# A gated graph network and an attention layer on one core: the work ahead of the first block in another order, W's extra columns in four steps, two products of v and W at a time, and both aggregation halves in one tick

## The chip, the cores and the metric

The kernel runs on one core of a Trainium2 chip. The metric is the device time of one execution in microseconds (us), lower is better. A profile is a recording of one execution; its span goes from the first to the last instruction, and the execution's own time lies a little above it.

## The reference

There are 64 graphs of 256 nodes with 256 features. A first layer runs three gated steps with a shared GRU cell and adds its input; a second layer is a masked attention over the neighbours. Each is followed by a layer norm.

```python
A = (adj != 0)
h = x
for i in range(3):
    m = h @ weight[i]
    aggr = einsum('bst,bsd->btd', A, m)
    h = gru_cell(aggr, h, w_ih, w_hh, b_ih, b_hh)
x = layernorm(x + h)
Wh = x @ W
e = leaky_relu((Wh @ a1)[:, :, None] + (Wh @ a2)[:, None, :], 0.2)
attn = softmax(where(adj > 0, e, -9e15), axis=2)
out = layernorm(x + attn @ Wh)
```

with `r = sigmoid(i_r + h_r)`, `z = sigmoid(i_z + h_z)`, `n = tanh(i_n + r * h_n)` and the new state `(1 - z) * n + z * h` in the cell.

## The kernel before

**Tiling.** P is 128, C = 2 chunks of 128 nodes or features, G = 2 graphs make a pair, so there are 32 pairs, and K = 4 chunks of nodes in a pair. The state of a pair is held turned, features on partitions: `hT` is 128 by 2 by 512. Since the adjacency comes first in the products, the kernel folds each `weight[i]` with `w_ih` into one weight, `wc[i]`, and aggregates the state itself.

**Three products for one.** To keep precision with the fast matmul type, an operand is cut into a high part, a low part and a cross part (`pieces`, tags H, L and D): `upper` on ScalarE (line 132), `lower` as a subtraction on VectorE or GpSimd (line 135), `cross` on VectorE (line 138). For a weight, `cut_weight` (line 140) also scales the low part on GpSimd (line 149), through a temporary `cut`. Ahead of clock 0 the temporary has three buffers; later, one (the tag `wh` of the pool `late`).

**Ticks.** The order of the work is written out by hand. There is a clock of ticks and a heap of steps that fall due: `at(t, step)` puts one in, `tick()` advances the clock and runs what is due, in order of the tick and then of entry. A step only issues instructions; each engine works through its own queue in that order, and semaphores make it wait for the others. The step's place in the tick order is thus its place in five queues at once.

**Blocks.** A block is layer i of pair p (lines 845 to 847); three pairs are under way at a time, in layers 0, 1 and 2, one after the other. `gates(p, i, lags)` (line 456) issues a block's products (line 468): for each half of the output columns r, n, z and t, each of 4, 6 or more matmuls of 512 columns from the H, L and D parts, into two PSUM banks `pga` and `pgb`, with one tick between the parts and one at the end, so 12 ticks in a block. ScalarE (line 473 and 475) and VectorE (line 477) bring the two banks together; sigmoid and tanh (line 486) and GpSimd (lines 494 to 504) finish the gate, and VectorE writes the new state (line 507).

**The front of the next block** is issued in the ticks of the one before: `front(p, i, t, pace)` (line 385). Its steps, for each half d: `turn` (transposes, lines 280 and 369), `split` (the high part on ScalarE, line 405), `rest` (the low part, line 135), `aggregate` (8 matmuls of 256 columns into a bank `pa`, line 439), `a_upper` (aH on ScalarE) and `a_rest` (aL and aD on VectorE). The step's tick is t plus its entry in `pace` plus d, so the two halves come one tick apart. Three more, `h_upper`, `h_lower` and `h_cross`, make hH, hL (on GpSimd) and hD. The paces are the tuples CLOSE, EARLY, FIRST, SECOND and THIRD at lines 832 to 836.

**PSUM** is one pool of eight banks (`bank`, line 106), taken in turn.

**Ahead of the first block** (lines 855 to 876) the clock runs from -100. Pair 0's x is turned and split, `rows_T` (line 214) turns the rows of w_ih and w_hh into `wihT` and the pieces `whh`, `square_T` (line 222) turns weight[0] into `wT`, `ones` (line 376) makes A of pair 0's adjacency, `fold` (line 234) makes `wc[0]` in four parts (two column ranges of 512 and 256, two halves d), and the front of pair 0 runs among them. Then the clock is set to 0 and the blocks begin. The folds of layers 1 and 2 and `attention_rows` are issued as steps in the first blocks: layer i's transposes at tick 8i-7, its halves 2 and 5 ticks later, and `attention_rows` at tick 17.

**attention_rows** (line 242) makes W's two extra columns, W times a1 and a2, and takes the mean over the rows from W: transposes of `gw` into `gwT` (line 226 and the copy at 229), four matmuls of 2 columns (line 247) with their copies (line 249), a memset of `mean` (line 251), two matmuls against it (line 254) and two subtractions (line 256). It is one step: all of it is issued together.

**attention(p, t)** (line 546) is issued in the ticks after a pair's last layer. `project(k)` (line 581) multiplies chunk k of the turned input by `gw`, 258 columns at the full type, into a bank `pwh` (line 589), at tick t+37+k. `spread(k)` (lines 598 and 600) takes it out of the bank one tick later, on ScalarE for k = 0 and 1 and on VectorE for 2 and 3. The last three pairs have their own version, `attention_last`.

Of the kernel before, what the change touches and what calls it, by code (L numbers as in the profile page):

```python
# [19 lines left out]
P = 128  # L20
# [7 lines left out]
def kernel(  # L28
# [60 lines left out]
    def at(t, step):  # L89
        clock[1] += 1  # L90
        heappush(pending, (t, clock[1], step))
# [14 lines left out]
    def bank(name):  # L106
        return psum.tile([P, 512], F32, tag="bank", name=name)
# [83 lines left out]
    w_n = []  # L191
# [30 lines left out]
    def square_T(src, name):  # L222
        pt = bank("pw")
        for e in range(C):
            for d in range(C):
                nc.tensor.transpose(pt[:, (e * C + d) * P:(e * C + d + 1) * P],
                                    src[:, d, e * P:(e + 1) * P], ident)
        dst = work.tile([P, GN], F32, tag="z", name=name)
        nc.scalar.copy(dst, pt)
        return dst.rearrange("p (e d) -> p e d", e=C)  # L230
# [8 lines left out]
                                 start=(e == 0), stop=(e == C - 1))  # L239
            cut_weight([t[:, d, o0:o1] for t in wc[i]], pt[:, :o1 - o0], f"{i}_{d}_{o0}")  # L240

    def attention_rows():
        gwT = square_T(gw, "gwT")
        for d in range(C):
            pt = bank("pw")
            for f in range(C):
                nc.tensor.matmul(pt[:, :2], gwT[:, f, d * P:(d + 1) * P], a_w[:, :, f],
                                 start=(f == 0), stop=(f == C - 1))
            nc.vector.tensor_copy(gw[:, d, D:], pt[:, :2])
        mean = late.tile([P, C, GN], F32, tag="vT", name="mean")[:, 0, :P]  # L250
        nc.vector.memset(mean, 1.0 / D)
        pt = bank("pw")[:, :D + 2]
        for d in range(C):
            nc.tensor.matmul(pt, mean, gw[:, d, :], start=(d == 0), stop=(d == C - 1))
        for d in range(C):
            nc.vector.tensor_sub(gw[:, d, :], gw[:, d, :], pt)


    class Pair:
# [125 lines left out]
    def front(p, i, t, pace):  # L385

        nm = f"{p}_{i}"
        by_dma = getattr(pairs.get(p), "by_dma", None) == i
        hi, lo, src = [None] * C, [None] * C, [None] * C
        if by_dma:  # L390
            hi, lo = pairs[p].hi, pairs[p].lo

        def turn(d):
            s = pairs[p]
            if i == 0:
                if p < FROM:
                    to_T(s.x, s.hT, d)
            else:
                src[d] = from_T(s.hT, d).rearrange("p (k n) -> p k n", k=K)

        def split(d):
            if i == 0:
                src[d] = nodes(pairs[p].x, d)
            hi[d] = work.tile([P, K, P], F32R, tag=f"hi{d}", name=f"hi{d}_{nm}", bufs=1)
            nc.scalar.copy(hi[d], src[d])

        def rest(d):
            lo[d] = work.tile([P, K, P], F32R, tag=f"lo{d}", name=f"lo{d}_{nm}", bufs=1)
            lower(nc.gpsimd if i == 0 and p else nc.vector, lo[d], src[d], hi[d])

        def stash():
            s = pairs[p]
            s.far = far.tile([P, C, GN], F32, tag="xT", name=f"xT_{p}")
            nc.sync.dma_start(s.far, s.hT)
        if i == 0:
            at(t + pace[0][0] + 3, stash)

        def h_upper():
            s = pairs[p]
            s.hc = pieces(work, [P, C, GN], nm, "h")  # L420
# [125 lines left out]
    def attention(p, t):  # L546
# [305 lines left out]

    def rows_inp(part):
        rows_T(part, lambda c, o0, o1, pt: evacuate(wih(c, o0, o1), pt))
    begin(0)
# [94 lines left out]
```

## Time and profile before

| What | Value |
|---|---|
| Median of 3 runs | 2078.24 us (2077.84 to 2080.43) |
| The profiled execution's own time | 2080.38 us |
| Its span | 2078.6 us |
| TensorE matmuls busy | 2048.2 us, 9844 instructions |
| TensorE weight loads busy | 1724.7 us |
| VectorE busy | 1787.8 us |
| ScalarE busy | 1659.6 us |
| GpSimd busy | 1616.4 us |
| Mean granted TensorE clock | 0.995 |
| Moved by DMA | 254.28 MB |

The page's parts, as the later sections use them: the first part gives the busy time of each engine (PE is TensorE's matmul, PEld its weight load, DVE VectorE, ACT ScalarE, POOL GpSimd, SP the queue that issues most DMAs); the second cuts the span into 40 slices, busy tenths of each, with the clock that TensorE was granted; the list of waits says for how long an engine sat idle ahead of a kind of instruction, whose end it waited for, how often, and the longest. A timeline row has its start and duration in us, the engine, the line in the kernel, what is written from what, the shapes and the number of merged instructions; in square brackets stands the idle time before it and who ended it. A matmul's busy time reaches into the next one's, so the distance from start to start is what a matmul costs. Two records of TensorE belong to one matmul at the full type (the folds and the products of v and W).

### The profile page before, as it was taken

Reading aid. Unit: us, or ns where it says so; the run is one execution under the profiler, and the core shown is the slowest. Engines: PE = TensorE matmul, PEld = TensorE weight load, DVE = VectorE, ACT = ScalarE, POOL = GpSimd, SP = SyncE. Lnnn points to the kernel's source line nnn. Section 1 sums busy time; section 2 is a strip of 40 time slices with the busy share of each in tenths; the row PEclk is TensorE's granted clock in tenths of the full one; section 3 lists DMA queues with packets and bytes.
Section 4 is the critical chain, followed back from the end, with each engine's and each line's share of the span. In section 5 each row is a group of like instructions: output and inputs, shape, how many; then the busy total and the mean of one; then the engine's idle time right before and its main releaser. Section 6 shows DMA issues by size and latency. Waiting matters only on the chain.

```text
span 2078.6 us, 31369 instructions
## 1 busy us (share of the span) xinstructions
PE 2048.2 (99%) x9844; PEld 1724.7 (83%) x9844; DVE 1787.8 (86%) x2896; ACT 1659.6 (80%) x3025; POOL 1616.4 (78%) x1114
## 2 busy tenths in 40 slices
PE   8999999999999999999999999999999999999996
PEld 6788888888888888888888888888888888888885
DVE  5676888898888898888898888898888898888887
ACT  4566888888888888888888888888888888888775
POOL 6777878787878787878787878787878787878763
PEclk9999999999999999999999999999999999999998
DMA  4112465664666665665665666665666665666221
GB/s 132 37 51 58 92 137 136 144 141 122 133 138 136 143 141 121 133 139 136 144 134 128 133 138 137 143 142 121 133 137 137 143 136 126 128 144 137 62 62 61
DMA packets 549734, 254.28 MB, mean 122 GB/s; under 512 B 372608, under 2 KB 541312, under 8 KB 549568
## 3 DMA queue, kind: packets, MB, share of 16 engines
q1 hardware_dynamic: 547776, 250.44, 54.9%
q8 instruction: 78, 1.28, 0.3%
q10 hardware_dynamic: 1616, 1.57, 0.2%
q14 instruction: 88, 0.72, 0.1%
q0 software_dynamic: 176, 0.27, 0.1%
HBM read 69.74 MB, written 33.55 MB: 50 GB/s over the span
## 4 chain that ended last, share of the span: by engine, by line
PE 96%; DVE 1%; POOL 1%; ACT 1%; DMA 0%; issue 0%; POOLq 0%; ACTq 0%; SPq 0%; DVEq 0%
PE pga L468 50%; PE pgb L468 25%; PE pa L439 9%; PE pwh L589 5%; PE po L673 5%; PE s L608 1%; PE pt L369 1%; PE pw L238 0%; DMA rows_hH<-in_L_gnn_w_hh_dram 0%; PE pwh L733 0%; PE po L796 0%; POOL wc2L_wc L149 0%; DVE cut L135 0%; PE pw L219 0%; POOL t L494 0%
## 5 line engine op out<-in xcount | busy, mean ns | idle before, releaser
L494 POOL TENSOR_TENSOR t<-hT,n 128x512 f32<-128x512 f32 x192 | 264.1, 1375 | 186.2 <-ACT n L486 185.9
L500 POOL TENSOR_TENSOR n<-n,r 128x512 f32<-128x512 f32 x192 | 318.5, 1659 | 74.8 <-ACT r L486 45.0
L504 POOL TENSOR_TENSOR n<-n,t 128x512 f32<-128x512 f32 x192 | 284.7, 1483 | 110.4 <-DVE t L477 100.6
L468 PE MATMUL pga<-hH,whhH_whh 128*128 128x512 f32 x1152 | 370.6, 403 | 0.0
L468 PE MATMUL pgb<-hD,whhD_whh 128*128 128x512 f32 x1152 | 356.9, 391 | 1.2 <-DVE hD L138 1.2
L468 PE MATMUL pga<-hL,whhL_whh 128*128 128x512 f32 x1152 | 356.9, 391 | 0.0
L495 POOL TENSOR_TENSOR t<-t,z 128x512 f32<-128x512 f32 x192 | 271.1, 1412 | 15.1
L135 POOL TENSOR_TENSOR hL<-hT,hH 128x1024 fp32r<-128x1024 f32 x96 | 260.5, 2714 | 9.1 <-ACT hH L132 9.0
L468 PEld LDWEIGHTS pgb<-hD,whhD_whh 128*128 128x128 f32 x1152 | 216.4, 188 | 49.0 <-DVE hD L138 1.5
L468 PEld LDWEIGHTS pga<-hL,whhL_whh 128*128 128x128 f32 x1152 | 216.5, 188 | 47.1
L468 PEld LDWEIGHTS pga<-hH,whhH_whh 128*128 128x128 f32 x1152 | 208.7, 189 | 35.0
L138 DVE SCALAR_TENSOR_TENSOR hD<-hH,hT 128x1024 fp32r<-128x1024 f32 x96 | 203.2, 2117 | 0.0
L486 ACT ACTIVATE n<-n,bi 128x512 f32<-128x512 f32 x192 | 139.0, 724 | 75.9 <-POOL n L504 75.6
L473 ACT ACTIVATE r<-pga 128x512 f32<-128x512 f32 x192 | 114.0, 594 | 103.6 <-PE pga L468 68.4
L439 PE MATMUL pa<-A,hi 128*128 128x256 f32 x768 | 194.3, 286 | 0.0
L439 PE MATMUL pa<-A,lo 128*128 128x256 f32 x768 | 192.0, 283 | 0.0
L507 DVE TENSOR_TENSOR hT<-t,n 128x512 f32<-128x512 f32 x192 | 191.1, 995 | 0.0
L477 DVE SCALAR_TENSOR_TENSOR r<-pgb,r 128x512 f32<-128x512 f32 x192 | 131.9, 687 | 60.5 <-PE pgb L468 32.2
L135 DVE TENSOR_TENSOR aL<-pa,aH 128x512 fp32r<-128x512 f32 x192 | 131.0, 682 | 59.6 <-ACT aH L132 59.5
L132 ACT ACTIVATE aH<-pa 128x512 fp32r<-128x512 f32 x192 | 116.1, 606 | 67.3 <-PE pa L439 67.3
L486 ACT ACTIVATE z<-z,b_sum 128x512 f32<-128x512 f32 x192 | 140.7, 733 | 19.6 <-DVE z L477 19.1
L473 ACT ACTIVATE t<-pga 128x512 f32<-128x512 f32 x192 | 115.6, 602 | 45.7 <-PE pga L468 41.9
(172 smaller groups left out, 5411.8 us busy)
## 6 DMA issues: line engine op xcount, KB each, us to landing
adj<-in_adj_dram SPq DMA_DIRECT2D x64, 512.0 KB, 3.8
second_h<-first_h SPq DMA_DIRECT2D x220, 128.0 KB, 4.1
x<-in_x_dram SPq DMA_DIRECT2D x32, 512.0 KB, 3.8
xT<-hT SPq DMA_DIRECT2D x32, 512.0 KB, 4.5
vT<-xT SPq DMA_DIRECT2D x32, 512.0 KB, 3.4
second<-first SPq DMA_DIRECT2D x116, 128.0 KB, 3.1
second<-v SPq DMA_DIRECT2D x116, 128.0 KB, 3.9
sc<-eT SPq DMA_DIRECT2D x232, 64.0 KB, 2.2
```

Source lines behind the costliest of these rows:

```text
L135: eng.tensor_sub(dst, src, hi.bitcast(F32))
L138: nc.vector.scalar_tensor_tensor(dst, hi.bitcast(F32), 1.0 + U, src, op0=ALU.mult, op1=ALU.subtract)
L439: nc.tensor.matmul(pt[:, g * N:(g + 1) * N], h[:, g * C + c, :], s.A[:, g, c, :], start=(n == 0), stop=(n == len(todo) - 1))
L468: nc.tensor.matmul(pt, w[:, d, o * P:(o + 1) * P], m[:, d, :], start=n in (0, ends + 1), stop=n in (ends, len(todo) - 1))
L473: nc.scalar.activation(dst, a, AF.Copy, scale=1.0 + U)
L477: nc.vector.scalar_tensor_tensor(dst, b, -1.0 / U, dst, op0=ALU.mult, op1=ALU.add)
L486: nc.scalar.activation(dst, dst, func, bias=bias)
L494: nc.gpsimd.tensor_sub(t, h, n)
L495: nc.gpsimd.tensor_mul(t, t, z)
L500: after(2, lambda r=r, n=n: nc.gpsimd.tensor_mul(n, n, r))
L504: after(1, lambda n=n, t=t: nc.gpsimd.tensor_add(n, n, t))
L507: after(lags[2], lambda n=n, t=t, h=h: nc.vector.tensor_add(h, t, n))
```

## The change

Four parts of the program are edited.

1. `attention_rows` becomes a tuple of four steps, `rows_turned`, `rows_times`, `rows_mean` and `rows_less`, which hand their tiles on in a dict. They are due at ticks 17, 18, 21 and 21.
2. In `front`, for layers 1 and 2 the steps `aggregate`, `a_upper` and `a_rest` aren't due before the tick of the second half's aggregation, so both halves' aggregations are issued in one tick; `a_upper` and `a_rest` keep their ticks or come in that one. Layer 0 keeps its paces.
3. In `attention`, `project(0)` and `project(1)` are issued at t+37, `project(2)` and `project(3)` at t+39. `spread` keeps its ticks, and `attention_last` isn't touched.
4. Ahead of the first block, every step is put into the heap with a tick of its own instead of standing between calls of `tick`, with other paces for pair 0's front, and what is not yet due at the end is moved to the new clock. The transposes of the second part of w_hh come before those of the second part of w_ih. Layer 1's fold does both halves at tick 3, and layer 2's starts at tick 7, with its halves at 12 and 16.

```diff
-    def attention_rows():
-        gwT = square_T(gw, "gwT")
+    rows_of = {}
+
+    def rows_turned():
+        rows_of["T"] = square_T(gw, "gwT")
+
+    def rows_times():
         for d in range(C):
-            pt = bank("pw")
+            pt = rows_of[d] = bank("pw")
...
-        mean = late.tile([P, C, GN], F32, tag="vT", name="mean")[:, 0, :P]
+
+    def rows_mean():
+        mean = rows_of["mean"] = late.tile([P, C, GN], F32, tag="vT", name="mean")[:, 0, :P]
...
+    def rows_less():
         for d in range(C):
-            nc.vector.tensor_sub(gw[:, d, :], gw[:, d, :], pt)
+            nc.vector.tensor_sub(gw[:, d, :], gw[:, d, :], rows_of["m"])
+    attention_rows = rows_turned, rows_times, rows_mean, rows_less
...
-                at(t + dt + d, lambda step=step, d=d: step(d))
+                dt = dt + d
+                if i and step in (aggregate, a_upper, a_rest):
+                    dt = max(dt, pace[0][3] + 1)
+                at(t + dt, lambda step=step, d=d: step(d))
...
         for k in range(K):
-            at(t + 37 + k, lambda k=k: project(k))
+            at(t + 37 + k // 2 * 2, lambda k=k: project(k))
             at(t + 37 + 1 + k, lambda k=k: spread(k))
...
-    front(0, 0, clock[0] + 1, ((0, 1, 2, 9, 11, 12), (7, 8, 13)))
-    tick(2)
-    rows_inp(wi_n[0])
-    tick()
-    rows_hid(wh_n[0])
-    tick()
-    rows_inp(wi_n[1])
-    tick()
-    rows_hid(wh_n[1])
-    wT = square_T(w_n[0], "wT_0")
-    nc.vector.tensor_add(b_sum, bi, bh)
-    tick()
-    ones(0)
-    load_adj(1)
-    tick()
-    for parts in PARTS:
+    front(0, 0, clock[0] + 1, ((0, 0, 1, 9, 11, 12), (5, 6, 10)))
+    for n, part in enumerate(wi_n):
+        after((3, 5)[n], lambda part=part: rows_inp(part))
+    for n, part in enumerate(wh_n):
+        after((4, 4)[n], lambda part=part: rows_hid(part))
+    after(5, lambda: wTs.update({0: square_T(w_n[0], "wT_0")}))
+    after(5, lambda: nc.vector.tensor_add(b_sum, bi, bh))
+    after(5, lambda: ones(0))
+    after(5, lambda: load_adj(1))
+    for n, o in enumerate(PARTS):
         for d in range(C):
-            fold(0, wT, d, (parts,))
-            tick(2)
-    tick(10)
-    load_x(1)
+            after((7, 14)[n] + 2 * d, lambda o=o, d=d: fold(0, wTs[0], d, (o,)))
+    after(17, lambda: load_x(1))
+    tick(25)
+    while pending and pending[0][0] <= clock[0]:
+        run_due()
+    moved = [(t - clock[0], n, step) for t, n, step in pending]
+    pending[:] = sorted(moved)
     clock[0] = 0
-    wTs = {}
...
-    for i in range(1, L):
-        after(8 * i - 7, lambda i=i: start_fold(i))
-        for d in range(C):
-            after(8 * i - 5 + 3 * d, lambda i=i, d=d: fold(i, wTs[i], d))
-    after(8 * L - 7, attention_rows)
+    for i, (t0, t1, t2) in enumerate(((0, 3, 3), (7, 12, 16)), 1):
+        after(t0, lambda i=i: start_fold(i))
+        after(t1, lambda i=i: fold(i, wTs[i], 0))
+        after(t2, lambda i=i: fold(i, wTs[i], 1))
+    for t0, step in zip((17, 18, 21, 21), attention_rows):
+        after(t0, step)
```

More of the change, by code (lines that the diff above doesn't have):

```diff
@@ L240, in fold @@
             cut_weight([t[:, d, o0:o1] for t in wc[i]], pt[:, :o1 - o0], f"{i}_{d}_{o0}")
-    def attention_rows():
-        gwT = square_T(gw, "gwT")
+    rows_of = {}
+    def rows_turned():
+        rows_of["T"] = square_T(gw, "gwT")
+    def rows_times():
         for d in range(C):
-            pt = bank("pw")
+            pt = rows_of[d] = bank("pw")
             for f in range(C):
-                nc.tensor.matmul(pt[:, :2], gwT[:, f, d * P:(d + 1) * P], a_w[:, :, f],
+                nc.tensor.matmul(pt[:, :2], rows_of["T"][:, f, d * P:(d + 1) * P], a_w[:, :, f],
                                  start=(f == 0), stop=(f == C - 1))
             nc.vector.tensor_copy(gw[:, d, D:], pt[:, :2])
-        mean = late.tile([P, C, GN], F32, tag="vT", name="mean")[:, 0, :P]
+    def rows_mean():
+        mean = rows_of["mean"] = late.tile([P, C, GN], F32, tag="vT", name="mean")[:, 0, :P]
         nc.vector.memset(mean, 1.0 / D)
-        pt = bank("pw")[:, :D + 2]
+        pt = rows_of["m"] = bank("pw")[:, :D + 2]
         for d in range(C):
             nc.tensor.matmul(pt, mean, gw[:, d, :], start=(d == 0), stop=(d == C - 1))
+    def rows_less():
         for d in range(C):
-            nc.vector.tensor_sub(gw[:, d, :], gw[:, d, :], pt)
+            nc.vector.tensor_sub(gw[:, d, :], gw[:, d, :], rows_of["m"])
+    attention_rows = rows_turned, rows_times, rows_mean, rows_less
     class Pair:
@@ L854, in rows_inp @@
         rows_T(part, lambda c, o0, o1, pt: evacuate(wih(c, o0, o1), pt))
+    wTs = {}
     begin(0)
     take_x(0)
-    front(0, 0, clock[0] + 1, ((0, 1, 2, 9, 11, 12), (7, 8, 13)))
-    tick(2)
-    rows_inp(wi_n[0])
-    tick()
-    rows_hid(wh_n[0])
-    tick()
-    rows_inp(wi_n[1])
-    tick()
-    rows_hid(wh_n[1])
-    wT = square_T(w_n[0], "wT_0")
-    nc.vector.tensor_add(b_sum, bi, bh)
-    tick()
-    ones(0)
-    load_adj(1)
-    tick()
-    for parts in PARTS:
-        for d in range(C):
-            fold(0, wT, d, (parts,))
-            tick(2)
-    tick(10)
-    load_x(1)
+    front(0, 0, clock[0] + 1, ((0, 0, 1, 9, 11, 12), (5, 6, 10)))
[8 more added lines that the diff above has]
+    for n, o in enumerate(PARTS):
+        for d in range(C):
+            after((7, 14)[n] + 2 * d, lambda o=o, d=d: fold(0, wTs[0], d, (o,)))
[5 more added lines that the diff above has]
+    pending[:] = sorted(moved)
     clock[0] = 0
-    wTs = {}
     def start_fold(i):
         wTs[i] = square_T(w_n[i], f"wT_{i}")
-    for i in range(1, L):
-        after(8 * i - 7, lambda i=i: start_fold(i))
-        for d in range(C):
-            after(8 * i - 5 + 3 * d, lambda i=i, d=d: fold(i, wTs[i], d))
-    after(8 * L - 7, attention_rows)
+    for i, (t0, t1, t2) in enumerate(((0, 3, 3), (7, 12, 16)), 1):
[4 more added lines that the diff above has]
+        after(t0, step)
     for n, (p, i) in enumerate(blocks):
```

## The prediction

> **What bounds the kernel now.** I read the page's first two parts, then the waits of TensorE, then its timeline at both ends of the longest waits.
>
> ```profile
> PE 2048.2 (99%) x9844; PEld 1724.7 (83%) x9844; DVE 1787.8 (86%) x2896; ACT 1659.6 (80%) x3025; POOL 1616.4 (78%) x1114
> PEclk9999999999999999999999999999999999999998
> ```
>
> TensorE is the bound from end to end; a gain must shorten its work, close a gap of it, or raise its clock. Its waits name nine gaps; these matter here:
>
> ```profile
> PE pw L247 <- ACT gwT L229: 2.3, 1, 2.3
> PE pw L219 <- DMA rows_hH<-in_L_gnn_w_hh_dram: 1.3, 1, 1.3
> PE pgb L468 <- DVE hD L138: 1.2, 1, 1.2
> PE pga L468 <- DVE aL L135: 1.0, 1, 1.0
> PE pw L238 <- ACT wT L229: 0.7, 1, 0.7
> PE pw L254 <- DVE mean L251: 0.4, 1, 0.4
> ```
>
> None repeats: all lie in the first 70 us, the stretch that the diff rewrites. (The three left out are x's first load, 6.0, and 7.5 us in the last pairs, which the diff leaves alone.) The timeline of TensorE around two of them:
>
> ```profile
> 24.93 0.47 PE L468 MATMUL pga<-aL,wc0L_wc 128*128 128x512 f32 x1
> 26.36 0.47 PE L468 MATMUL pga<-aL,wc0L_wc 128*128 128x512 f32 x1 [0.95 <-DVE aL L135]
> 27.99 0.74 PE L468 MATMUL pgb<-hD,whhD_whh 128*128 128x512 f32 x2 [1.17 <-DVE hD L138]
> ...
> 31.05 1.05 PE L468 MATMUL pga<-hL,whhL_whh 128*128 128x512 f32 x2
> 31.91 0.70 PE L468 MATMUL pgb<-hD,whhD_whh 128*128 128x512 f32 x2
> ```
>
> The reader is to see two things. A busy duration overlaps the next, so loss is read from start to start: 24.93 to 26.36 is 1.43 where a product normally takes 0.23. And after the gaps, two products start 0.86 us apart from the next two (31.05 to 31.91) where 0.455 is normal. The stretches of 3.41 us show why (columns: busy us of PE, PEld, DVE, ACT, POOL, then the granted clock):
>
> ```profile
> 25.25:28.66 3.41, 1.29 (x5) 0.76 (x5) 3.41 (x6) 2.17 (x4) 3.25 (x3) 1.00 0.00 0
> 28.66:32.07 3.41, 3.41 (x12) 2.73 (x11) 1.66 (x2) 0.00 (x0) 0.42 (x1) 0.50 0.35 77
> ...
> 66.21:69.62 3.41, 1.44 (x10) 1.32 (x11) 0.46 (x3) 0.59 (x1) 2.13 (x2) 1.00 0.00 0
> 69.62:73.03 3.41, 3.41 (x12) 2.73 (x11) 1.89 (x4) 0.59 (x1) 0.00 (x0) 0.50 0.00 0
> ```
>
> Each stretch in which TensorE worked under half the time is followed by one at half clock. So an early gap is paid twice.
>
> [...] a stretch with 2.73 of 3.41 busy, from 15.01, was followed by full clock. [...] the half-clock stretches count as 3.41 of 3.41 busy. [...] both halves of pa were complete by about 21.6, yet aH began at 22.79, behind wc0H at 22.51. [...] hD[...] took 1.22 us at 26.72 and 2.12 on average; I use both ends.
>
> **The change part by part.** I compare the order of instructions of the two programs with durations from the trace.
>
> *First block.* TensorE's order is unchanged up to the first aL product; what moves is who stands ahead on the other queues.
> - ScalarE now does hH before the first wc0H: it starts about 16.0, in a gap that ScalarE has anyway (2.07 us before wc0H at 18.02). It does both aH before the 256-wide wc0H: about 20.7 and 21.7 instead of 22.79.
> - GpSimd: hL (2.37) goes ahead of the first wc0L. The whhL steps end between 18.4 and 19.4, hL thus between 20.8 and 22.2[...]; needed at 23.64. The two 512-wide wc0L (1.5 each) end by 23.7 to 25.2; the second is needed at 25.16.
> - VectorE: wc0D ends at 21.73; then hD (1.22 to 1.9), which before stood last, then aL, aD, aL, aD at 0.61 each. hD ends at 22.9 to 23.6 (needed 25.4, before 27.94); the second aL at 24.8 to 25.4 (needed 25.16, before 26.21); the last aD at 25.4 to 26.0 (needed 26.07). The four 256-wide cut steps (0.34 start to start) now come after, and are wanted only by the n product, microseconds later.
> - SP: its order stays; A comes some 0.8 us earlier as the second lo (1.14) leaves its place, so adj and x of pair 1 are issued no later than 18.66 and 19.14.
>
> Removed: 1.43-0.23 = 1.20 and (27.99-26.36)-0.23 = 1.40; left: 0 to 0.3. The gap at hH's DMA (1.3) and wT (0.7) stay: hL's rows move ahead of aL's on TensorE, but hH's load lands at 10.95 and wT's copy at 15.96 in either order.
>
> *Folds of W.* Layer 1's second fold comes at once after the first, layer 2's later. The TensorE work is the same; the cover is the pair's products. The temporary of a cut has one buffer, so each cut waits for GpSimd: four rounds of about 2.2, 1.3, 2.2, 1.3 = 7 us, and n's combination on VectorE is queued behind them, holding its PSUM bank. The folds start near 28.4 and run 5.2 us (twice the 2.6 from 32.44 to 35.02), to 33.6; the first is copied by 30.9, so the rounds end near 37.9. The last bank comes round after four transposes, 18 products and eight aggregation matmuls: 33.6+0.4+4.1+1.0 = 39.1. Cost nothing, with 1.2 us of cover; without it, what is over, up to 1 us.
>
> *W's extra columns.* Before, transposes, copy, products, mean and subtraction stand together, and gwT's copy waits for a z buffer (GpSimd's t, 1.5 us): last transpose 65.19, next matmul 67.79, so 2.60-0.11 = 2.49, and 0.4 for mean. In the new order, ten matmuls (four transposes and six products, 1.8 us) lie between gwT's transposes and its use, enough for a copy of 0.59 and its queue. The mean's memset (0.17) now stands on VectorE behind r's combination, and its two matmuls follow the n product directly: 0 to 0.7 lost, I take 0.6.
>
> Stalls: removed 1.20+1.40+2.49+0.4 = 5.5; left 0.6; **4.9 us gained**, between 3.5 and 5.5.
>
> *Clock.* Work in a half-clock stretch takes double, so each costs 3.41/2 = 1.7 us. With at most 0.6 us idle at a place, neither stretch is near the rows that tripped it: **3.4 us gained**; 1.7 if one trips still, 0 if both.
>
> *Products and aggregation halves together.* The products after a group of eight aggregation matmuls start 0.47, 0.46, 0.46 us apart per two, then 0.455: 0.03 us lost per break. A pwh group plus three such pairs takes 1030.17 to 1032.42 = 2.25, less 3x0.455 and four matmuls at 0.216: 0.02 lost. In the new order there are 57 fewer pwh breaks and 35 fewer aggregation breaks (where layer 1's first half stood next to the s2 transposes, it leaves one break there): 57x0.02+35x0.03 = 2.2. The trace shows no group of double length between products in the steady stretch, so this is bounded by 0 (the recovery doubles too) and 2.2; I take **1.5**. A slower end is excluded unless a bank or input is late, which is a rival below. spread stays on its ticks, so the second product's bank is held one tick longer; TensorE has no bank wait in the trace, and the bank comes round only after seven others.
>
> Sum: 4.9+3.4+1.5 = 9.8 us, against the profiled execution's 2080.38 (span 2078.6 and 1.8 around): 2070.6. That run is 2.1 above the median of three, 2078.24, about one half-clock stretch; if the median run had one fewer, it would gain 8.1 and end at 2070.1. I predict **2070.0**.
>
> **Rivals.**
> 1. *The stall moves on.* hL, wc0L and aL are within 0.3 us of late[...]. If two of them wait about 1.2 us in one stretch and the clock halves once, 2x1.2+1.7 = 4.1 come back: 2074.1. For: GpSimd is busy 3.25 of 3.41 us there. Against: hL gains at least 1.2 us.
> 2. *The gain is hidden anyway*: the pair's elementwise chain, not TensorE, ends the first blocks, and what TensorE gains it waits later. Only the 1.5 remain: 2076.7. Against: no TensorE wait from 73 us to the last pairs.
> 3. *Slower*: the first aggregation half now comes one tick (about 2.3 us) later, so ScalarE and VectorE get two halves at once, and aL or aD misses the next block. Per turn, layer 1's last aD ends at 1049.80 and its first product starts at 1053.36, layer 2's at 1072.32 against 1075.16: slack 2.8 to 3.6. Only the earlier half moves, so it would take a further 2.8 us of delay; at 0.3 us beyond, in 62 turns, 18.6 lost: 2070.0+18.6 = 2088.6. It turns the sign from 0.16 us a turn.
> 4. *It doesn't group*: excluded, the instruction order shows it.
>
> **How the numbers follow.** Forecast 0.76 (2066.5 to 2074); rival 1 0.10; rival 2 0.08; rival 3 0.06. The low end is all upper bounds: 5.5+3.4+2.2 = 11.1 off 2078.24 is 2067.1, and 0.6 for the runs' own spread. The high end takes in rival 1's edge, 2074.5. A measurement tells 0.2%, 4.2 us, from no change: faster means below 2074.1. Forecast and a third of rival 1 are faster (0.79); the rest of rival 1 and rival 2 the same (0.15); rival 3 slower (0.06).
>
> **What would show it.** Right: no TensorE wait on aL, hD or gwT over 0.4 us; no 0.50 clock between 20 and 100 us; aH near 20.7; hL done before 22.3; product steps back at 0.455 after a group of sixteen with one break of 0.03. Wrong: a wait on wc0L or hL near 25, on mean near 70 over 1 us, a half-clock stretch there, or any TensorE wait repeated every turn.

## The result and the profile after

| | Median, us | Runs |
|---|---|---|
| before | 2080.01 (2077.82 to 2082.54) | 14 |
| after | 2075.66 (2074.62 to 2078.32) | 14 |
| ratio | 0.998 (95%: 0.9972 to 0.9988) | |

The changed kernel is faster by 4.35 us, a fifth of a per cent. The forecast was 2070.0, from 2066.5 to 2074.5, with a gain of 8 to 10 us: the sign is right, the size half of it or less. (The kernel before, which had a median of 2078.24 in the three runs known ahead, has 2080.01 in fourteen.) The profiled execution after took 2075.49, its span 2073.7. Each median below is set against runs of before on the same chip; a difference of means is given with its standard error.

In the kernel after, `gates` is at L480 (before L468), `aggregate` at L448, the products of v and W at L601, the rows steps at L251 to L264. The page's first lines after:

```profile
PE 2045.1 (99%) x9844; PEld 1721.6 (83%) x9844; DVE 1786.0 (86%) x2896; ACT 1659.6 (80%) x3025; POOL 1615.7 (78%) x1114
PEclk9999999999999999999999999999999999999998
```

TensorE is the bound as before; its busy time counts half-clock stretches as busy (3.41 of 3.41 us in the one from 2047.95, below) and so tells little of the change. Its waits after, without x's first load and two in the last pairs:

```profile
PE pt L796 <- ACT sc L784: 4.4, 7, 1.5
PE pw L219 <- DMA rows_hH<-in_L_gnn_w_hh_dram: 1.3, 1, 1.3
PE pw L260 <- DVE mean L257: 1.2, 1, 1.2
PE pga L480 <- POOL wc0L_wc L149: 0.9, 1, 0.9
PE pw L238 <- ACT wT L229: 0.7, 1, 0.7
PE pw L219 <- DMA rows_hL<-in_L_gnn_w_hh_dram: 0.4, 1, 0.4
```

The waits on aL, hD and gwT are gone. Two of about 1 us stand there now, on wc0L (new) and on mean (0.4 before), and a shorter one on hL's DMA. Their places in TensorE's timeline:

```profile
23.55 0.48 PE L480 MATMUL pga<-aL,wc0L_wc 128*128 128x512 f32 x1
24.93 0.50 PE L480 MATMUL pga<-aL,wc0L_wc 128*128 128x512 f32 x1 [0.91 <-POOL wc0L_wc L149]
25.27 0.62 PE L480 MATMUL pgb<-hD,whhD_whh 128*128 128x512 f32 x2
...
69.54 0.62 PE L480 MATMUL pgb<-hD,whhD_whh 128*128 128x512 f32 x2
71.32 1.11 PE L260 MATMUL pw<-gw,mean 128*128 128x258 f32 x4 [1.16 <-DVE mean L257]
```

From start to start, 24.93 - 23.55 - 0.23 = 1.15 us are lost at the first and 71.32 - 69.54 - 0.46 = 1.32 at the second. The stretches of 3.41 us, windows from here on, are those at whose borders the granted clock changes: in the trace of before at 15.01, 28.66, 32.07, 69.62, 73.03 and 2045.94, thus 4, 1, 11, 1 and 578 times 3.413 us apart. The ones that hold the two waits and two of the tail (busy us of PE, PEld, DVE, ACT, POOL; then the clock, and the DMA's share and GB/s):

```profile
23.83:27.24 3.41, 2.50 (x13) 1.94 (x13) 3.21 (x7) 2.21 (x4) 3.17 (x4) 1.00 0.02 5
27.24:30.65 3.41, 3.41 (x14) 2.17 (x13) 0.06 (x1) 1.28 (x2) 1.18 (x1) 1.00 0.52 154
...
68.20:71.60 3.40, 2.24 (x12) 1.66 (x12) 2.97 (x5) 1.43 (x3) 2.57 (x2) 1.00 0.00 0
71.60:75.00 3.40, 3.40 (x16) 2.82 (x15) 2.53 (x5) 1.81 (x4) 2.19 (x2) 1.00 0.00 0
...
2044.54:2047.95 3.41, 1.98 (x11) 1.09 (x11) 2.81 (x10) 3.40 (x13) 0.00 (x0) 1.00 0.00 0
2047.95:2051.36 3.41, 3.41 (x9) 2.76 (x10) 2.38 (x8) 2.01 (x7) 0.00 (x0) 0.50 0.00 0
```

Neither early gap is followed by half clock any more. In the tail, the work behind the last block's first product, the stretch of 1.98 is.

**Where the time went.** The first hH product of each block dates the blocks. (Block 3 lies behind everything that is rewritten at the start; block 95 is the last.)

| First product of | before | after | saved |
|---|---|---|---|
| block 0 | 22.99 | 21.61 | 1.37 |
| block 1 | 55.39 | 50.73 | 4.67 |
| block 3 | 103.50 | 95.63 | 7.87 |
| block 95 | 2016.22 | 2009.06 | 7.16 |
| end of TensorE | 2068.51 | 2063.44 | 5.06 |

So the first blocks save 3.30 and 3.20, 6.5 in all where 8.3 was forecast; the steady stretch *loses* 0.7 instead of gaining 1.5; and the tail gives 2.1 back. The 1.37 ahead of block 0 was not forecast. Four questions follow: whether the merges gain or lose, whether the first blocks' gain holds in every execution, what the tail is, and what the two new waits cost.

### The profile page after: what moved, and what is told of

Read it like the earlier page. It is cut to its first block, busy times and chain, and to the rows that moved or that the text cites. A ratio compares the mean times of both kernels' runs of the same rounds, so it can differ in the third digit from the quotient of the medians.

```text
span 2073.7 us, 31342 instructions
## 1 busy us (share of the span) xinstructions
PE 2045.1 (99%) x9844; PEld 1721.6 (83%) x9844; DVE 1786.0 (86%) x2896; ACT 1659.6 (80%) x3025; POOL 1615.7 (78%) x1114
## 4 chain that ended last, share of the span: by engine, by line
PE 97%; DVE 1%; ACT 1%; POOL 1%; DMA 0%; issue 0%; POOLq 0%; ACTq 0%; SPq 0%; DVEq 0%
PE pga L480 51%; PE pgb L480 25%; PE pa L448 9%; PE po L685 5%; PE pwh L601 5%; PE s L620 1%; PE pt L378 1%; PE pw L238 0%; PE po L808 0%; DMA rows_hH<-in_L_gnn_w_hh_dram 0%; PE pwh L745 0%; POOL whhL_whh L149 0%; POOL wc0L_wc L149 0%; ACT sc L784 0%; DVE hD L138 0%
## 5 line engine op out<-in xcount | busy, mean ns | idle before, releaser
L480 PE MATMUL pga<-hH,whhH_whh 128*128 128x512 f32 x1152 | 367.3, 400 | 0.1
L480 PE MATMUL pgb<-hD,whhD_whh 128*128 128x512 f32 x1152 | 356.7, 391 | 0.0
L480 PE MATMUL pga<-hL,whhL_whh 128*128 128x512 f32 x1152 | 356.6, 391 | 0.0
L480 PEld LDWEIGHTS pgb<-hD,whhD_whh 128*128 128x128 f32 x1152 | 216.3, 188 | 47.4
L480 PEld LDWEIGHTS pga<-hL,whhL_whh 128*128 128x128 f32 x1152 | 216.2, 188 | 47.2
L480 PEld LDWEIGHTS pga<-hH,whhH_whh 128*128 128x128 f32 x1152 | 208.3, 189 | 36.8 <-ACT r L485 0.9
L448 PE MATMUL pa<-A,lo 128*128 128x256 f32 x768 | 189.2, 282 | 0.0
L448 PE MATMUL pa<-A,hi 128*128 128x256 f32 x768 | 189.1, 283 | 0.0
L489 DVE SCALAR_TENSOR_TENSOR n<-pgb,n 128x512 f32<-128x512 f32 x192 | 130.8, 681 | 23.7 <-ACT n L487 23.7
```

The source lines that it names most:

```text
L480: nc.tensor.matmul(pt, w[:, d, o * P:(o + 1) * P], m[:, d, :], start=n in (0, ends + 1), stop=n in (ends, len(todo) - 1))
L489: nc.vector.scalar_tensor_tensor(dst, b, -1.0 / U, dst, op0=ALU.mult, op1=ALU.add)
```

## The experiments

**1. The parts alone.** Each merge can be taken from the change or put back by itself. The pairs of products are one line:

```diff
-            at(t + 37 + k, lambda k=k: project(k))
+            at(t + 37 + k // 2 * 2, lambda k=k: project(k))
```

The kernel before with the new order and the rows steps, no merge:

> The kernel before with the new order ahead of the first block and W's extra columns in four steps; products of v and W and the aggregation halves stay one per tick. Theory A (the gain lies in the first two blocks alone, the merges give nothing in the steady stretch): the medians differ by -4 to -7 us from before, at or up to 1.5 us below the changed kernel; the first product of block 3 starts 6 to 8 us earlier than before's 103.50, and the distance stays as it is to block 90. The prediction's sum says -8.3 (4.9 of stalls and 3.4 of clock). Rival B (the merges do gain about 1.5, and something else eats it): this kernel is slower than the changed one by about 1.5 us.

Measured: median 2073.56 against 2079.62, ratio 0.997 (0.9958 to 0.9981); mean -5.7 +- 0.35. Block 3 starts at 96.13, 7.37 ahead of before (0.51 of it ahead of block 0), and block 90 still 7.39 ahead.

The kernel before with the pairs of products alone:

> The kernel before with only the products of v and W two chunks at a time. The prediction's sum says -0.6 to -1.2 us (57 breaks at 0.02, 0 at the least). Theory A: +0.5 to +2 us, because a group of eight records has a longer recovery (about 0.025 us per pair, 29 pairs) and the n product behind the second pair waits now and then for r's PSUM bank (0.9 us in two waits of the changed kernel's trace). In the trace: the first products after a group of eight start further apart than 0.455 in sum by about 0.03 more than twice the loss of a group of four, and a wait of the weight load at line 468 on r's copy at line 473 comes up.

Measured: 2082.75, ratio 1.0013 (1.0006 to 1.002); mean +2.8 +- 0.34. **Pairing loses.** The timeline of before around two products, then that of the pairs:

```profile
1030.17 1.03 PE L589 MATMUL pwh<-gw,vT 128*128 128x258 f32 x4
1030.85 0.81 PE L468 MATMUL pga<-aL,wc0L_wc 128*128 128x512 f32 x2
1031.49 0.63 PE L468 MATMUL pgb<-hD,whhD_whh 128*128 128x512 f32 x2
1031.96 0.62 PE L468 MATMUL pgb<-aD,wc0D_wc 128*128 128x512 f32 x2
```

```profile
1030.44 1.91 PE L589 MATMUL pwh<-gw,vT 128*128 128x258 f32 x8
1031.99 0.82 PE L468 MATMUL pga<-aL,wc0L_wc 128*128 128x512 f32 x2
1032.64 0.63 PE L468 MATMUL pgb<-hD,whhD_whh 128*128 128x512 f32 x2
1033.12 0.62 PE L468 MATMUL pgb<-aD,wc0D_wc 128*128 128x512 f32 x2
```

From the group's start to the second pair of products behind it, less the 0.455 of the first, four records cost 1.32 - 0.455 = 0.865 and eight 2.20 - 0.455 = 1.745, twice as much: there was no break to save. The next step is 0.48 instead of 0.47, and a few more are 0.005 to 0.01 above 0.455. By the starts of the blocks a turn (three blocks, one of each layer) is 0.03 longer. And the n product behind the second pair now meets a bank that ScalarE, which copies the r products out of it, has not yet read. The weight loads' waits between 100 and 1990 us have this line:

```profile
PEld pga L468 <- ACT r L473: 1.3, 3, 0.6
```

The bank is near its limit without pairs too: in 13 of the 17 traces of kernels with one product per tick, though not in the first of before, a product of v and W waits once or twice for the same copy, 0.2 to 0.9 us of weight-load wait in all. By its trace the kernel with pairs loses 1.5 us from block 0 to block 95, about half of it in longer turns and the rest in turns with such waits.

Both halves in one tick alone:

> The kernel before with only both aggregation halves of layers 1 and 2 in one tick. The prediction's sum says -1.05 us (35 breaks at 0.03). Theory A: -0.6 us (about 0.02 per turn of three blocks, 32 turns), within what the runs of one kernel differ by. The rival of the prediction (aL or aD late every turn) says slower by up to 18 us, and a TensorE wait on VectorE's line 135 or 138 that repeats.

Measured: 2079.28, ratio 0.9998 (0.9989 to 1.0006); mean -0.3 +- 0.33. In the trace each block of layer 1 is 0.02 shorter, 27 of 27; no TensorE wait on aL or aD repeats, so the forecast's slower rival is out.

The changed kernel without the pairs:

> The changed kernel with the products of v and W one per tick again. Theory A: 0.5 to 2 us faster than the changed kernel (about 2074.5), and no weight load at line 480 waits for r's copy at line 485. The prediction's sum says 0.6 to 1.2 us slower than the changed kernel. If the 2.1 us that the changed kernel loses in the last 60 us belong to the pairs, this kernel's last products stand 7 us ahead of before's; if it is the phase of the half-clock stretches, the number of such stretches after 2030 us varies from run to run, whichever merges are in.

Measured: 2074.45, ratio 0.9973 (0.9963 to 0.9984); mean -5.3 +- 0.53 against the -4.15 +- 0.54 of the changed kernel, a difference that these errors don't settle. The n product no longer waits for r's copy; a product of v and W does once, for 0.2. Its last block starts 6.78 ahead of before's, not 7: a single wait on the low part of an x took 1.3 us in block 16 of this trace.

All four products in one tick (`at(t + 37, ...)`), on the kernel before:

> The kernel before with all four products of v and W of a pair issued in one tick (sixteen records in a row); the copies out of the banks keep their ticks. The prediction's sum would say -1.7 us (86 breaks at 0.02). Theory A (the recovery after full-type products grows with their number, and banks are held longer, so r's or n's next product waits): +2 to +6 us, by 0.05 to 0.1 us in each block of layer 0 from recovery, and a repeated weight-load wait on ScalarE's copy of r or n beyond that.

Measured: 2081.38, ratio 1.0004 (0.9997 to 1.0011); mean +1.4 +- 0.45. Here my theory was wrong: a turn is 0.04 us *shorter*, of which the sixteen records give 0.015 (3.495 where four times four cost 4 x 0.877 = 3.51) and the products behind them the rest. Two turns lost (0.6 and 0.2), and it waits 1.2 us for r's bank as the pairs do. A longer group thus does not recover worse in proportion; of the three lengths tried, only eight shows the loss. (The mean is still 1.4 up: in the trace the tail took 55.33 us instead of 52.29, with a wait on vT of 4.0 instead of 3.1.)

**2. The start, in halves.** The rows steps alone on the kernel before:

> The kernel before with only W's extra columns in four steps, at ticks 17, 18, 21 and 21. Theory A: the stalls of 2.3 and 0.4 us at gwT and mean go, one of about 1.2 at mean comes, and the half-clock stretch near 69.6 us goes: block 2's first product comes 3.2 us earlier than before's 84.26 where the stretch is gone, 1.5 where one stays, and the medians differ by -1.5 to -3.2. The prediction's sum says -4.0 (2.49 + 0.4 - 0.6 + 1.7). Rival (the gap at gwT is hidden anyway by what follows): 0, with a new TensorE wait before 84 us.

Measured: 2079.41, ratio 0.9998 (0.999 to 1.0007); mean -0.5 +- 0.45. The one execution traced says why so little: 0.6 us of wait at gwT is left and mean's has grown to 1.2, of 2.7 in all before; the half clock behind them is gone, and from block 1 to block 2 it saves 2.35; but the tail takes 54.36 us instead of 52.29 and gives 2.1 of that back.

The new order and folds alone, W's extra columns in one step:

> The kernel before with only the other order ahead of the first block and the other places of the folds of layers 1 and 2; W's extra columns stay one step, products and halves one per tick. Theory A: the waits on aL and hD (1.0 and 1.2) go, one of 0.6 to 0.9 on wc0L comes, and no half clock follows near 28 us: block 1 starts 3.3 to 4.2 us earlier than before's 55.39, block 2 no further, and the medians differ by -2.5 to -4.2. The prediction's sum says -4.3 (1.20 + 1.40 + 1.7). e5 and this one should add up to the kernel with both, -6.1.

Measured: 2075.12, ratio 0.9975 (0.9965 to 0.9986); mean -4.7 +- 0.45. Block 1 starts 4.57 earlier (1.26 of it ahead of block 0). Against the expectation block 2 gains too, and starts 7.67 earlier, as with both edits: gwT's wait falls from 2.3 to 0.7 without the split, and no half clock follows. That the other places of layer 2's fold do this is likely, but no run moves them alone. Each edit alone removes most of that gap, so they may not be counted separately. The means do add: -0.5 - 4.7 = -5.2 against -5.7.

**3. The clock apart from the stall.** Products that nobody reads fill the gap in the kernel before:

```diff
             pt = bank("pw")
+            if d == 0:
+                for _ in range(8):
+                    nc.tensor.matmul(pt, whh[0][:, 0, :P], whh[0][:, 0, :512], start=True, stop=True)
```

> The kernel before, with eight products of 512 columns (0.227 us each, 1.8 in all) that nobody reads put into the gap in which TensorE waits for gwT's copy, into the bank that the next product overwrites. This parts the clock from the stall: the stall of 2.3 us stays, filled. Theory A and the prediction: no half-clock stretch near 69.6 us, block 2 starts 1.4 to 1.7 us earlier than before's 84.26, and the medians differ by -1 to -1.7. Rival (the half clock doesn't come from this gap, or costs nothing because TensorE isn't the limit there): 0 or slower by up to 0.5.

Measured: 2078.70, ratio 0.9999 (0.9991 to 1.0007). The half clock came all the same:

```profile
65.93:69.35 3.42, 2.50 (x15) 1.86 (x14) 0.46 (x3) 0.58 (x1) 2.29 (x2) 1.00 0.00 0
69.35:72.76 3.41, 3.41 (x11) 2.74 (x11) 1.59 (x4) 0.59 (x1) 0.00 (x0) 0.50 0.00 0
```

The stretch counts 2.50 busy, and the kernel after has one of 2.50 without a penalty. But 1.05 of it is the record of eight 2-column products at 67.67, 0.13 each, where one of 512 columns costs 0.23; products of real size run only to about 67.1 and from 69.12. This run was too weak to answer, so both gaps of the start were filled (four ahead of the last aL, four ahead of the first hD, ten at gwT, two at mean):

> The kernel before with its early gaps filled by products of 512 columns that nobody reads: four ahead of the last aL product and four ahead of the first hD product of the first block, ten in the gap at gwT's copy, two ahead of the mean's products. The stalls stay, the clock's reason goes: the earlier run with eight at gwT alone left half the window there without real work (the 2-column matmuls are recorded long and do almost nothing), and its half-clock stretch came all the same. The prediction's sum says -3.4 us. Theory A, sharpened: in the traced executions both stretches are there, but in others, where the windows fall differently, a gap is shared between two windows and trips none, so the mean is -1 to -2.5; in the trace no half clock between 20 and 100 us and block 2 starts 2.5 to 3.4 us earlier than 84.26. Rival (half clock there costs nothing): 0.

Measured: 2078.96, ratio 0.9995 (0.9987 to 1.0004); mean -0.9 +- 0.26. No half clock between 20 and 100 us, block 2 starts at 80.17; but 1.14 of these 4.1 us lie ahead of block 0, where nothing differs, and the mean gains less than a third of the 3.4 forecast. The traces of before were evidently not all alike, and it was traced four times more, unchanged:

> The kernel before, unchanged, traced once more (first of four). Theory A, sharpened: where full clock is first granted at 13.9 to 15.4 us, both half-clock stretches come, near 28 and 69 us, and block 2 starts at 83.6 to 84.4; where it is granted at 8.5 to 10.5, the first or both are missing and block 2 starts 2.5 to 4.2 us earlier. Rival (the stretches come always): both in all four, block 2 at 82.5 or later.

> The kernel before, unchanged, second trace of four; theories and numbers as for the first.

> The kernel before, unchanged, third trace of four; theories and numbers as for the first.

> The kernel before, unchanged, fourth trace of four; theories and numbers as for the first. Over the four, theory A wants at least one without the first stretch, unless all four windows fall alike (1 in 16 if both cases are equally likely).

| Trace of before | full clock from | half clock near 28, 69 | block 0 | block 3 | time |
|---|---|---|---|---|---|
| the first | 15.01 | yes, yes | 22.99 | 103.50 | 2080.38 |
| 1 | 10.29 | yes, yes | 21.75 | 102.52 | 2079.65 |
| 2 | 8.82 | no, yes | 21.79 | 100.97 | 2078.07 |
| 3 | 9.40 | no, yes | 21.76 | 100.88 | 2078.54 |
| 4 | 15.38 | yes, yes | 23.50 | 104.00 | 2081.09 |

Two of four lack the first stretch, never the second. The time of the first grant doesn't tell which: number 1 has an early one and both stretches, against the expectation. In number 2 the windows lie so:

```profile
22.47:25.88 3.41, 2.46 (x11) 1.51 (x10) 3.41 (x8) 1.74 (x5) 3.17 (x4) 1.00 0.06 20
25.88:29.30 3.42, 2.28 (x12) 1.92 (x13) 3.38 (x3) 0.88 (x2) 2.15 (x2) 1.00 0.02 5
29.30:32.71 3.41, 3.41 (x15) 2.17 (x14) 0.27 (x1) 1.33 (x3) 0.00 (x0) 1.00 0.46 154
...
63.43:66.85 3.42, 1.21 (x9) 1.13 (x10) 0.46 (x3) 0.59 (x1) 2.37 (x2) 1.00 0.00 0
66.85:70.26 3.41, 3.41 (x11) 2.74 (x12) 1.44 (x4) 0.59 (x1) 0.00 (x0) 0.50 0.00 0
```

and in number 1:

```profile
23.94:27.35 3.41, 1.69 (x9) 1.04 (x8) 3.41 (x6) 2.13 (x4) 3.17 (x4) 1.00 0.00 0
27.35:30.77 3.42, 3.42 (x12) 2.75 (x11) 1.95 (x2) 0.00 (x0) 0.71 (x1) 0.50 0.16 53
```

Same waits, same kernel: in number 2 the gap fell on the border of two windows, left them 2.46 and 2.28 us of work and cost nothing more; in number 1 it fell within a window, left 1.69 and was paid twice (from block 0 to block 1, 31.06 and 32.64 us). The windows keep no fixed place against the program: by the table, a border lies 1.15, 1.22 and 1.29 us ahead of block 0's first product in the three traces with the first stretch (the first, 1 and 4), and 2.73 and 2.12 in the two without (block 0 less the first grant, modulo 3.413). The prediction took each gap's place from its one trace and didn't ask how else the windows could fall.

**4. What the tail is.** A dose of work in the middle (seven or fifteen products that nobody reads, in one block of pair 16) asks what a delay is worth at the end:

> The kernel before with seven more products of 512 columns that nobody reads, 7 x 0.227 = 1.6 us of TensorE work, ahead of the first product of one block in the middle (pair 16, layer 0). It measures what 1.6 us in the steady stretch are worth at the end, as the pairs of products lost 1.5 there by their trace but 2.8 by the mean of the runs. If the windows of the clock fall at random against the kernel's start, every delay is paid once: mean +1.6. If they don't, a shift of half a window also changes how many half-clock stretches the tail meets: +2.5 to +3.2, as for the pairs, whose loss then needs no further cause.

> As the dose of seven, with fifteen: 15 x 0.227 = 3.4 us, a whole window of 3.41. The tail meets the windows then as it does before, so both theories say +3.4 in the mean; anything from +2.9 to +3.9. With the dose of seven it says whether the tail's length goes by the remainder of the delay: there more than 1.6, here not more than 3.4.

Measured: 1.6 us of work cost +2.4 +- 0.34 (ratio 1.0013, 1.0006 to 1.0019), 3.4 us +4.1 +- 0.35 (1.002, 1.0014 to 1.0027). Both are 0.7 to 0.8 above the work, so the means don't say that a part of a window costs more than a whole one. The traces are plainer. Take the time from the last block's first product to the first half-clock stretch of the tail, of which only the remainder by 3.41 counts, and the time from that product to TensorE's end, over the nineteen traces whose tail has no added work:

| Remainder, us | Last product to end, us | Traces |
|---|---|---|
| 0.89 to 1.34 | 54.14 to 54.38 | 7, after among them |
| 1.70 to 2.41 | 52.17 to 52.29 | 8, before among them |
| 2.65 | 55.33 | 1, with a wait for vT of 4.0 instead of 3.1 |
| 2.83 to 3.25 | 53.05 to 53.37 | 3 |

The same work takes 2 us more or less as the windows fall: each of the seven in the first row has three half-clock stretches ahead of TensorE's end, each of the eight in the second has two. All five traces of before lie between 1.70 and 2.83. Filling the tail's gaps tests it, on a version that takes the two waits away. That version has neither merge, issues mean's memset with the first rows step, and scales one low part on ScalarE:

```diff
+        if name == "0_1_0":
+            nc.scalar.activation(dst[1], tmp, AF.Copy, scale=1.0 / U)
+        else:
+            nc.gpsimd.tensor_scalar(dst[1], tmp, 1.0 / U, None, op0=ALU.mult)
```

> The version that the runs so far point to: the other order ahead and the four steps, one product and one half per tick, and the two waits that the new order leaves taken away: the memset of mean is issued with the first of the four steps, four ticks earlier, and the scaled low part of the second 512-wide cut of layer 0's weight is made on ScalarE instead of GpSimd. Theory A: the waits on mean (1.1) and wc0L (0.6 to 0.9) go, block 3 starts 1.5 to 1.8 us earlier than with both edits alone (96.13), median about 2072. Rival (something else is late next, as hL's DMA or aH on ScalarE, which now waits behind the scaling): 2073.5, as without.

Measured: 2073.10, ratio 0.9969 (0.9957 to 0.9981); mean -6.2 +- 0.31. Both waits are gone and block 3 starts at 94.21, 1.9 us earlier than with them (96.13), but the mean against before moves only from -5.7 to -6.2, and the median stays a us above the 2072 expected. Its tail takes 54.15 us, where the version with the waits took 52.17.

> The version with both waits covered, and the gaps of the last two pairs filled with products of 512 columns that nobody reads: eleven ahead of the last pair's first transposes of vT (a gap of 3.05 us), four, four and six ahead of the transposes of sc (gaps of 1.10, 1.22 and 1.45). Theory (the tail's length is set by half-clock stretches): few or none between 2030 and 2058 us, 51.5 to 52.5 us from the first product of the last block to TensorE's end instead of 54.15, and the mean 0.7 to 2 us below the same version without the fillers. Rival (the tail is bound by ScalarE and VectorE): no shorter, or longer by up to 1 as the fillers stand ahead of work.

> The version with both waits covered, unchanged, beside the one with the tail filled, so that both share a chip and the runs of before. The earlier run says 2073.1, -6.2 in the mean against before; this one should say -5.6 to -6.8. Its trace is a second one of its tail: 52.2 to 52.4 us where the windows fall 1.7 to 2.4 us after the last block's first product (modulo 3.41), 54 to 54.4 where at 0.9 to 1.35.

Measured side by side: with the tail filled 2071.10, ratio 0.9958 (0.9946 to 0.9971), mean -8.65 +- 0.73; without 2073.21, 0.9968 (0.9956 to 0.998), mean -6.7 +- 0.30. The trace without fell at a remainder of 1.07 and took 54.27 us in the tail, as was expected for that remainder; the one with them took 52.13, with one half-clock stretch instead of three. The timelines of the last products (without, with):

```profile
2046.09 3.35 PE L809 MATMUL po<-wh,sc 128*128 128x256 f32 x8
2049.50 1.89 PE L809 MATMUL po<-wh,sc 128*128 128x256 f32 x8
2056.07 5.20 PE L809 MATMUL po<-wh,sc 128*128 128x256 f32 x16
```

```profile
2045.97 3.38 PE L816 MATMUL po<-wh,sc 128*128 128x256 f32 x8
2049.41 1.89 PE L816 MATMUL po<-wh,sc 128*128 128x256 f32 x8
2055.89 3.62 PE L816 MATMUL po<-wh,sc 128*128 128x256 f32 x16
```

Sixteen records take 5.20 in a tail with half clock and 3.62 with full. The fillers, 25 products of no use, take 2.0 +- 0.7 us off (five runs against six). So the tail's half clock is real cost and can be had back; a favourable place of the windows does as much without fillers (52.17 in the table). This is the fastest version of all, 4.5 us below the changed kernel by the means against before.

## Why the prediction was half right

**Stalls, forecast 4.9: about 3.1.** What was to go went, 5.5 by start-to-start. What was to stay at 0.6 was 1.15 + 1.32 = 2.5, which leaves 3.0; the trace has 6.5 less 3.4 of clock. In the first block most dates held: aH began at 20.27 (forecast 20.7), hL ended at 20.88 (20.8 to 22.2; in before it takes 2.37 to 2.97 us, 2.89 at the median), the second aL stood ready at 23.76. The failed step is the pair of dates "the two 512-wide wc0L (1.5 each) end by 23.7 to 25.2; the second is needed at 25.16", of which the text then counted 0 to 0.3. Four steps stand in a row on GpSimd from 20.96; the first took 2.35 us, not 1.5, and the second ended at 24.88, still within the range:

```profile
18.48 2.40 POOL L135 TENSOR_TENSOR hL<-hT,hH 128x1024 fp32r<-128x1024 f32 x1
20.96 6.09 POOL L149 TENSOR_SCALAR wc0L_wc<-cut 128x512 fp32r<-128x512 f32 x4
```

But TensorE wanted it at 23.55 + 0.23 = 23.78. The 25.16 was read from a trace in which block 0 began at 22.99; here it began at 21.61. Over the traces with the new order the wait goes with this start: 0.91 us at 21.61, 0.88 at 21.73 (the order alone), 0.56 at 22.48 (no merges), none at 22.97 (no pairs; there the two steps took 1.49 and 1.61). So most of the 1.37 that came for nothing ahead of block 0 was lost again 2 us later.

At mean, "0 to 0.7 lost, I take 0.6": hD, an instruction of 2.12 on average in before, took 3.28 here beside GpSimd's hL, and the memset, in order behind it, came at 71.01:

```profile
65.96 3.28 DVE L138 SCALAR_TENSOR_TENSOR hD<-hH,hT 128x1024 fp32r<-128x1024 f32 x1
...
70.36 0.68 DVE L489 SCALAR_TENSOR_TENSOR r<-pgb,r 128x512 f32<-128x512 f32 x1
71.01 0.17 DVE L257 MEMSET mean<- 128x128 f32 x1
```

Taking both waits away gave 1.9 us in the trace, 0.5 up to block 1 and 1.4 from there to block 2, which shows that they were on the path. What made the first wc0L step take 2.35 us and this hD 3.28 is not shown.

**Clock, forecast 3.4: 3.4 between the two traces, some 2.9 on average.** From block 0 to block 3 the five traces of before take 80.51, 80.77, 79.18, 79.12 and 80.50, mean 80.02; the first, on which the sum was built, lies 0.5 above. After takes 74.02. The step "each stretch in which TensorE worked under half the time is followed by one at half clock" was right for the windows of that trace, and wrong as a price per gap: the second gap was paid always in before, the first in three traces of five. Nor is half the time the border: a window with 1.98 us of work was followed by half clock in the trace of after (from 2044.54), one with 1.55 was not where both gaps were filled (from 2036.49). How much of this term reaches the end is not shown by the changed kernel. Where the gaps were filled and all else stayed, the trace took 77.56 from block 0 to block 3, 2.5 below the mean of before, but 53.37 in the tail, 1.0 above it, and the runs gained 0.9 +- 0.26.

**Groups, forecast 1.5 gained: 0.7 lost in the trace.** This step failed in its sign for the pairs. The 0.02 per break was an upper bound, read from one group plus six products, and I took two thirds of the sum although only the aggregation's break was measured cleanly. "The trace shows no group of double length between products in the steady stretch" was not true either: the eight-record po groups of the same stretch were there to be read (behind the one at 1066.65 the next steps are 0.65 and 0.47, behind the eight records from 1030.44 of the pairs 0.65 and 0.48). The pairs cost 1.5 in the trace of their own and 2.8 +- 0.34 in the runs; the halves gain 0.02 per turn, 0.6 in all. In the changed kernel's trace a turn is thus only 0.007 longer, 0.2 in all; the other 0.5 lies in two single turns (0.4 and 0.3), and a wait for r's copy in a single turn costs kernels without pairs up to 0.8 as well. "The bank comes round only after seven others" overlooked that two banks a tick bring it round sooner; "no bank wait in the trace" held for that one trace, and 13 of 17 have one.

**Tail, not in the sum.** That it is the same in both programs was taken without a word. It is the same work, and 54.38 against 52.29, with three half-clock stretches against two.

The trace's sum: 1.37 ahead of block 0 (full clock from 10.19, which before has too, from 8.82 to 10.29, in three of five) + 3.1 + 3.4 - 0.7 - 2.1 = 5.1, as TensorE's ends show. Against the forecast's 9.8: 1.8 less from the stalls, 2.2 less from the groups, 2.1 lost in the tail, and 1.4 of luck at the start the other way. Against the mean of the five traces of before, which the prediction didn't have, the same sum is 0.75 + 6.0 - 0.5 - 2.0 = 4.2, as the means of the runs say (4.15 +- 0.54).

**The rivals.** The stall moved on, as the first said, but without half clock. The second is out: in the trace without merges, what the start gains stands unchanged to block 90 (7.37 and 7.39). So is the third. The fourth was rightly excluded.

**Open:** why the pairs cost 1.3 more in the runs than in the steady stretch of their trace. Their tail fell at a remainder of 0.89 (54.14 us), which would be enough; but the dose of seven, whose trace fell at 1.11, cost only 0.8 too much in the runs, and so did the dose of a whole window, which fell at 1.78. Why eight records are worse than four or sixteen stays open too, and what decides about a stretch of 1.5 to 2.5 us of work.

## What to carry to other kernels

Read a gap's clock penalty from several traces, and price it by how the windows can fall across it, not by the one that you have: the first gap here was followed by half clock in three traces of five. Before counting breaks saved by a longer group, find a group of that length in the trace and read what it costs to the fifth product behind it. Take the dates at which work is needed from several traces too: here TensorE waited 0.91 us for wc0L where block 0 began at 21.61, and not at all where it began at 22.97. A gain at the start of a kernel that is bound by one engine can be lost again in the tail, which took 52.29 us here with two half-clock stretches and 54.38 with three: filling its gaps with products of no use was worth 2.0 +- 0.7 us, half as much as the whole change.

## What the runs showed of the hardware

- Over the twenty traces, stretches of 3.41 us at full clock with up to 1.44 us of recorded TensorE work were always followed by half clock, those with more than 2.50 never. Between, both came, and the recorded work didn't tell which: 2.50 was (eight products in the gap at gwT, from 65.93) and was not (after, from 23.83), 1.98 was (after, from 2044.54), 1.97 was not (the third trace of before, from 2036.92), 2.24 was (four products in one tick, from 2052.91), 1.55 was not (both gaps filled, from 2036.49). Gaps far shorter than a window were enough: two of 0.95 and 1.17 us in before, in the stretch from 25.25 with 1.29 of work.
- The windows lie differently against the same program from run to run: full clock was first granted between 8.82 and 15.38 us in five traces of before, and a border lay 1.15 to 2.73 us ahead of block 0.
- Groups of four, eight and sixteen full-type records of 258 columns cost 0.877, 1.754 and 3.495 us; of these only the eight made a turn longer than the four, by 0.03 us.
- The tail of the same instructions took 52.17 to 52.29 us in eight traces with two half-clock stretches and 54.14 to 54.38 in seven with three.
- 25 products without a use, put into the tail's gaps, made the kernel 2.0 +- 0.7 us faster.
